# Reordering the fill of a two-layer graph kernel: small vectors' transpose, an affine step, half features, weight sums

## The chip, the cores and the metric

The kernel runs on one core of one Trainium2 chip. Its engines are TensorE (PE in the profile; PEld is its weight load), VectorE (DVE), ScalarE (ACT), GpSimd (POOL), and the DMA queues, of which SyncE (SP) issues most. The metric is the device time of one execution in microseconds (us). All line numbers are those of the kernel before; the changed kernel's run lower by one from line 588 on and drift further behind the edits.

## The reference

There are 64 graphs with 256 nodes and 256 features each (x), and a 0/1 adjacency matrix of 256 x 256 per graph. Two layers follow each other, everything in float32.

Layer 0: `h = gat(x, W1, a1)`, `h = gat(h, W2, a2)`, where `gat` projects `Wh = h @ W`, forms scores `leaky_relu(Wh @ a[:F] + (Wh @ a[F:]).T)` masked by the adjacency, takes a softmax over `axis=1`, and multiplies by `Wh`. Then `h = layernorm(x + h) * g + b`, `ff = relu(h @ w_ff1 + b_ff1) @ w_ff2 + b_ff2` with 1024 hidden values, and `layernorm(h + ff) * g + b`.

Layer 1: q, k from Wq, Wk, eight heads of 32, scores and a softmax; for each relation r of four, `out += (attn * (adj == r)) @ v_r` (with a 0/1 adjacency only relations 0 and 1 are ever selected); an output projection Wo, a residual and a layernorm; a gelu feed-forward of 1024 hidden values, a residual and a layernorm.

## The kernel before

**Staging.** The core takes two graphs at a time, a pair u of 32 (NG). A pair's rows lie as four blocks of 128 (T = 4; blocks 0 and 1 are the first graph of the pair, 2 and 3 the second). The main part is a loop of turns (`turn`, from L1276): turn u does the attention and second feed-forward of pair u, and beside it the layer 0 feed-forward of pair u+1 and the graph attention of pair u+2. Ahead of the loop stands the fill (L1613 to L1754), which brings pair 0 to the start of its attention and pair 1 to its first layernorm. It is written out by hand, and so is the order of instructions on PE, SP, DVE, ACT and POOL there (`manual_schedule`). Each engine works its queue in that order, and a wait at the head of a queue holds what is behind it. In turns with a following pair, PE, SP, DVE and ACT are ordered by hand too; POOL's place is then set by where its instructions stand, with some tied behind a mark (`behind`).

**Seven products for eight.** Large products are done with seven block products in place of eight (`hidden_seven` L909, `HiddenOut` L998, `Projections` L1047). Each needs sums of weights, made once by POOL (`made`, L628, one sum of two tiles per step), and sums or differences of data, made by DVE. Results pass through a PSUM bank to which a later product is added, so that the later one may only start when the earlier has been read: product 7 follows 6 in its bank, 6 follows 1, 4 follows 7, and 3 follows 5 (which itself takes the bank of 2 in the hidden layers and the projections). `taken` reads by a copy on ACT, or, where the place has begun, by an add on DVE (L948, L1079, L1036). In the step names of the fill a digit is a product, a or b a half of the hidden blocks, r, c, d and s an activation.

**Layernorm.** `moments` (L860) takes statistics on DVE, `norm` (L870) makes 1/std on POOL (rs, L877 and L878), `offsets` (L883) makes -mean/std on DVE (nm, L885), and `applied_norm` (L887) applies both on ACT (L895). The affine step with gain and bias (`affine`, L898: `times` L904, `plus` L907, both DVE) is put on the residual rows alone. For the features that the next product reads, gain and bias are folded into the weights: `scaled` (POOL, L646) multiplies the weights by the gain, and `shift_products` (L634) and `shift_added` (L640) bring the bias through the weights into the next bias. These need gains and biases as columns, so eight small vectors are loaded as 28 rows and transposed by PE in `columns` (L487; the transpose is L499, the copy L500).

**Features.** PE transposes rows to features in PSUM (`turned`, L512), and ACT or DVE copies them (`features`, L521). `with_ones` (L708) has POOL write ones into one feature row that carries the bias. A pair's features hold the first graph in columns 0 to 255 and the second in 256 to 511. `Projections.sums` (L1058) makes four differences from both graphs' features.

**Buffers.** Ordinary PSUM banks (`bank`, L423) turn in a ring of six.

**The order around the change.** At the head, PE transposes the small vectors (L588), then the first graph's adjacency (L1627), then alternates projections of pair 0 (`project`, L1631) with sums of the first bias through wf1 (L1632). ACT's queue begins with a check of the adjacency values (`checked`, L1625), which waits for that matrix's DMA. In the middle, the affine step of pair 0 (L1716) stands between two groups of sums; DVE does it ahead of the adds of product 6. At the end (L1745 to L1753) both graphs' rows are normed, transposed, copied as whole features, given their ones, and only then turn 0 begins with its differences and products.

Of the kernel before, what the change touches and what calls it, by code (L numbers as in the profile page):

```python
# [9 lines left out]
F32 = mybir.dt.float32  # L10
# [6 lines left out]
P = 128  # L17
# [368 lines left out]
def narrow_path(  # L386
# [13 lines left out]
    nc = tc.nc  # L400
# [4 lines left out]
    KB = F // P  # L405
# [81 lines left out]
    def columns(vs, name, queue, tag):  # L487

        ns = [v.shape[0] // P for v in vs]
        rows = work.tile([P, KB, TN], F32, tag=tag, name=f"{name}r", bufs=1)[:, 0, 0:P]  # L490
        t = const.tile([P, sum(ns)], F32, name=name)
        at, views = 0, []
        for v, n in zip(vs, ns):
            queue.dma_start(rows[at:at + n, :], v.rearrange("(c p) -> c p", p=P))
            views.append(t[:, at:at + n])
            at += n
        def turned_columns():
            ps = bank(f"{name}p")
            nc.tensor.transpose(ps[:, :at], rows[:at, :], ident[:at, :at])  # L499
            nc.vector.tensor_copy(t, ps[:, :at])  # L500
            return views

        return turned_columns
# [75 lines left out]
    def idle(n):  # L579
# [5 lines left out]
    idle(5)  # L585
    gwe = gat_weights()
    wf1 = weight(g_wf1, "wf1")
    lg1, lb1, bf1, lg2, lb2, lg3, lb3, b1 = columns(  # L588
        (g_g1, g_b1, g_bf1, g_g2, g_b2, t_g1, t_be1, t_b1), "cols", nc.scalar, "q")()

    wqk = const.tile([P, KB, 2 * F], F32, name="wqk")
    for k in range(KB):
# [35 lines left out]
    def made(ops, n=4):  # L628
        for _ in range(n):
            o, x_, y_, op = next(ops)  # L630
            nc.gpsimd.tensor_tensor(o, x_, y_, op)
# [63 lines left out]
    def behind(*names):  # L695

        stack = ExitStack()
        for n in names:
            stack.enter_context(tc.issue_after(mark[n].ins))
        return stack  # L700
# [346 lines left out]
    class Projections:  # L1047
# [3 lines left out]
        def __init__(s, u, hT):  # L1051
            s.u = u
            s.qk = work.tile([P, KB, 2, TN], F32, tag="q", name=f"qk{u}", bufs=1)
            s.v = work.tile([P, T, 2 * F], F32, tag="v", name=f"v{u}", bufs=1)
            s.h = [[hT[k][:, b * N:(b + 1) * N] for b in range(G)] for k in range(KB)]
            s.one, s.two, s.begun = {}, {}, set()

        def sums(s):  # L1058
            tt = work.tile([P, HPB, NB * N], F32, tag="e", name=f"tq{s.u}").rearrange("p a n -> p (a n)")
# [213 lines left out]
        if left:  # L1273
            next(left[0], None)

    def turn(y_, x_, z):  # L1276
        Y, X, Z = (g.get(u) for u in (y_, x_, z))
        hT, y = Y["hT"], Y["y"]
        quads = [(b, m) for b in range(G) for m in range(KB)]
# [40 lines left out]
        def moved(moves, n):  # L1320
            for _ in range(n):
# [2 lines left out]
        order = tc.manual_schedule(engines={getattr(mybir.EngineType, n) for n in  # L1324
                                            ("PE", "SP", "DVE", "Activation")[:4 if X else 2]})
        with order:
            p.sums()
            if X:
                n = X.pop("n")
                if y_:  # L1330
                    offsets(*n)
                p("q2 v2 q1 v1")
                if not y_:
                    offsets(*n)
                applied_norm(X["y"], *n, [0, 1, 2, 3])
                p("q5")
            else:
                p("q1 v1 q2 v2 q5")
# [113 lines left out]
                shares(1)  # L1452
            if not y_:
                with behind("low"):
                    made(w2m, 4)
            out_(0)
            if Z:
# [155 lines left out]
    with tc.manual_schedule(engines={getattr(mybir.EngineType, n) for n in  # L1613
                                     ("PE", "SP", "DVE", "Activation", "Pool")}):
        a, b = g[0], g[1]

        def spread(m):
            m.scores(0)
            m.scores(1)

        def powers(m):
            m.exp(0)
            m.exp(1)

        checked(0, g[0]["aq"], squares[:, 2:4].rearrange("p a n -> p (a n)"))  # L1625
        onlys = [only_row(n) for n in ("wqk", "wv")]
        turn_a = early_adjacency_of(0, 0)  # L1627
        turn_a()
        ps = bank("bf1sp")
        for t in range(T):  # L1630
            project(0, [t])  # L1631
            shift_products(ps, wf1, range(2 * t, 2 * t + 2), lb1)  # L1632
        shift_added(ps, range(FB), bf1)
        turn_a = early_adjacency_of(0, 1)
        turn_a()
        first_scores(0)
        spread(a["m"])
        powers(a["m"])
        turn_b = [early_adjacency_of(1, 0)]
        px = turned(b["y"], "xT1")  # L1640
        b["xT"] = features("xT1", px, (nc.scalar.copy,) * 2)
        pqk = row_products(wqk, "wqk", onlys[0])
        for k in range(G):
            a["m"].masks(k)
        a["m"].shares()
        a["m"].scaled(WH)
        scaled(wf1, lg1)
        made(wf1m, 2)
        first_sums(0)
        scaled_rows(wqk, *pqk)  # L1650
        nc.vector.tensor_tensor(wv[:, :, 1, :], wv[:, :, 1, :], wv[:, :, 0, :], ALU.subtract)
        second_scores(0)
        turn_b.append(early_adjacency_of(1, 1))
        spread(a["m"])
        a["m"].exp(0)
        project(1, range(NB))
        a["m"].exp(1)
        project(1, range(NB, T))
        for k in range(G):
            a["m"].masks(k)  # L1660
        a["m"].shares()
        made(wf1m, 2)
        made(wf2m, 1)
        first_scores(1)
        a["m"].scaled(F)
        for t in turn_b:
            t()
        second_sums(0, (0,))
        n0 = norm(0, 0, a["y"], range(NB))
        b["m"].raw(0)  # L1670
        b["m"].raw(1)
        checked(1, g[1]["aq"], squares[:, 2:4].rearrange("p a n -> p (a n)"))
        second_sums(0, (1,))
        mv = moments(0, 0, a["y"], range(NB, NB + 1))
        offsets(*n0)
        n1 = norm(0, 0, a["y"], range(NB, T), mv=mv, rest=range(NB + 1, T))
        applied_norm(a["y"], *n0, range(NB))
        offsets(*n1)
        applied_norm(a["y"], *n1, range(NB, T))
        b["m"].leaky(0)  # L1680
        pv = row_products(wvf, "wv", onlys[1])
        ph = turned(a["y"], "h1T0", range(NB))
        ps = bank("b1sp0")
        shift_products(ps, w1, range(0, 2), lb3)
        idle(2)
        turned(a["y"], "h1T0", range(NB, T), ph)
        shift_products(ps, w1, range(2, 4), lb3)
        a["hT"] = features("h1T0", ph, (nc.scalar.copy, nc.vector.tensor_copy))
        load_x(2)
        load_rows(2)  # L1690
        load_adjacency(2)
        steps = first_hidden(0)
        b["m"].leaky(1)
        shift_added(ps, range(0, 4), b1)
        steps("2a")
        powers(b["m"])
        steps("1a")
        b["m"].masks(0)
        steps("2b 1b")
        b["m"].masks(1)  # L1700
        b["m"].shares()
        for rb, v in shifts:
            nc.gpsimd.tensor_add(rb, rb, v)
        made(wf2m, 3)
        steps("5a 5b")
        b["m"].scaled(WH)
        scaled_rows(wvf, *pv)
        nc.vector.tensor_tensor(brow[:, 3], brow[:, 3], brow[:, 2], ALU.subtract)
        biased(wqk, brow[:, 0:2])
        biased(wvf, brow[:, 2:4])  # L1710
        made(wqkm, 4)
        steps("3a 3b")
        ps = bank("b1sp1")
        shift_products(ps, w1, range(4, 6), lb3)
        first_sums(1)
        affine(a["y"], rg1, rb1)  # L1716
        shift_products(ps, w1, range(6, FB), lb3)
        shift_added(ps, range(4, FB), b1)
        scaled(w1, lg3)
        made(w1m, 2)  # L1720
        steps("6a ra 6b rb")
        second_scores(1)
        steps("7a sa 7b sb 4a 4b")
        first = HiddenOut(0, 0, a["y"], a["h1"], wf2s, out_sums(0, 0))
        first.sums(1, 2)
        spread(b["m"])
        powers(b["m"])
        first(1)
        first.sums(4)
        first(2, 5)  # L1730
        b["m"].masks(0)
        first.sums(3)
        first(6)
        b["m"].masks(1)
        b["m"].shares()
        b["m"].scaled(F)
        made(wvm, 4)
        first(3)
        n0 = norm(0, 1, a["y"], range(NB))
        first(7)  # L1740
        offsets(*n0)
        applied_norm(a["y"], *n0, range(NB))
        first(4)
        n1 = norm(0, 1, a["y"], range(NB, T))
        second_sums(1, (0,))  # L1745
        ph = turned(a["y"], "h2T0", range(NB))
        offsets(*n1)
        applied_norm(a["y"], *n1, range(NB, T))
        second_sums(1, (1,))
        turned(a["y"], "h2T0", range(NB, T), ph)  # L1750
        mv = moments(1, 0, b["y"], range(NB))
        a["hT"] = with_ones(features("h2T0", ph, (nc.scalar.copy,) * 2))
        b["n"] = norm(1, 0, b["y"], mv=mv)  # L1753
        late.append((a["y"], rg2, rb2))  # L1754
    with tc.manual_schedule(engines={mybir.EngineType.PE, mybir.EngineType.SP}):
        for u in range(NG):
            turn(u, u + 1, u + 2)


    c = work.tile([P, 4], F32, tag="mv", name="checks")  # L1760
# [51 lines left out]
```

## Time and profile before

| | |
|---|---|
| three runs | 2962.96, 2960.92, 2951.9 us; median 2960.92 us |
| profiled execution | 2953.9 us, span 2952.3 us, granted PE clock 0.998 |
| PE busy | 2921.4 us, 99% of the span |
| DVE busy | 2612.6 us, 88% |
| ACT busy | 1898.3 us, 64% |
| POOL busy | 629.3 us, 21% |
| chain that ended last | PE 96%, DVE 2%, ACT 1% |

A busy PE is one with a matmul under way; matmuls are pipelined, so the sum of single durations is larger than the time they take together. The chain that ended last is followed back from the last instruction, at each step to what released it. Three parts of the span differ: the fill up to some 102 us, the turns, and the last turn from about 2850 us on, where fewer pairs are left to work beside each other. The change touches the fill and, by two weight sums, the first turn.

### The profile page before, as it was taken

The numbers are of one execution on the slowest core, as the hardware profiler recorded it, in microseconds if no ns is written. First come the engines' busy times: TensorE is split into PE (matmuls) and PEld (weight loads), VectorE is DVE, ScalarE is ACT, GpSimd is POOL, SyncE is SP. The second block draws the span as 40 slices with busy tenths as digits, with TensorE's granted clock in tenths as the row PEclk, the third lists the DMA queues.
The fourth block names the chain that finished last, engine by engine and source line by source line (L and its number), as shares of the span: only waits on it lengthen the run. The fifth ranks groups of instructions, "written<-read, shape, count | busy, mean of one in ns | idle before, by whom it ended". The sixth has DMA issues, their size and how long they took to land.

```text
span 2952.3 us, 58648 instructions
## 1 busy us (share of the span) xinstructions
PE 2921.4 (99%) x22206; PEld 2501.8 (85%) x22206; DVE 2612.6 (88%) x5027; ACT 1898.3 (64%) x3982; POOL 629.3 (21%) x930
## 2 busy tenths in 40 slices
PE   8999999999999999999999999999999999999997
PEld 7788888888888888888888888888888888888876
DVE  5889899989989898999898998899998989988987
ACT  5566666676676666666766766766667667667652
POOL 4212221122121122221221211222212212112211
PEclk9999999999999999999999999999999999999999
DMA  5011111111111111111111111111111111111000
GB/s 152 12 31 32 38 32 34 24 40 32 37 29 23 38 32 39 32 32 24 39 32 37 31 28 31 35 37 34 30 23 40 32 37 32 29 30 33 18 8 16
DMA packets 408020, 99.27 MB, mean 34 GB/s; under 512 B 357834, under 2 KB 407220, under 8 KB 407732
## 3 DMA queue, kind: packets, MB, share of 16 engines
q1 hardware_dynamic: 406332, 94.13, 14.8%
q8 instruction: 178, 2.92, 0.4%
q0 software_dynamic: 1056, 1.05, 0.1%
q14 instruction: 110, 0.90, 0.1%
q10 hardware_dynamic: 344, 0.28, 0.0%
HBM read 56.78 MB, written 16.78 MB: 25 GB/s over the span
## 4 chain that ended last, share of the span: by engine, by line
PE 96%; DVE 2%; ACT 1%; issue 0%; POOL 0%; DMA 0%; POOLq 0%; DVEq 0%; ACTq 0%
PE yf L1028 26%; PE h1a L939 15%; PE h1b L939 11%; PE po L1144 8%; PE v L1095 6%; PE qk L1095 6%; PE sp L1116 4%; PE hpp L840 4%; PE xpp L773 4%; PE ygp L851 4%; PE yop L851 4%; PE zo L1147 2%; PE rows L782 1%; DMA first<-in_adj_dram 0%; DVE st L866 0%
## 5 line engine op out<-in xcount | busy, mean ns | idle before, releaser
L1125 ACT ACTIVATE e<-sp 128x512 f32<-128x512 f32 x512 | 270.9, 611 | 71.4 <-issue 42.8
L1129 DVE TENSOR_TENSOR ea<-e,aT 128x1024 f32<-128x1024 f32 x256 | 310.9, 1216 | 1.8 <-ACT e L1125 1.8
L895 ACT ACTIVATE y<-y,nm,rs 128x256 f32<-128x256 f32 x442 | 235.1, 592 | 63.7 <-DVE nm L885 62.9
L948 DVE TENSOR_TENSOR h<-h1a,h 128x512 f32<-128x512 f32 x293 | 197.3, 682 | 80.7 <-PE h1a L939 77.3
L951 ACT COPY h<-h1b 128x512 f32<-128x512 f32 x293 | 175.2, 599 | 124.8 <-PE h1b L939 123.2
L957 ACT ACTIVATE h<-h,cols 128x256 f32<-128x256 f32 x512 | 221.9, 502 | 36.2 <-DVE h L948 32.0
L735 POOL COPY hT<-yt 32x256 f32<-32x256 f32 x244 | 211.5, 867 | 143.3 <-DVE yt L718 128.6
L1082 ACT COPY qk<-qk 128x512 f32<-128x512 f32 x128 | 74.4, 581 | 238.9 <-PE qk L1095 238.1
L866 DVE BATCH_NORM_STATS2 st<-y 128x6 f32<-128x256 f32 x512 | 208.6, 408 | 5.6
L877 POOL TENSOR_SCALAR rs<-mv 128x4 f32<-128x4 f32 (+1 forms) x134 | 41.5, 309 | 806.8 <-DVE mv L867 445.8
L1036 DVE TENSOR_TENSOR y<-yf,y 128x256 f32<-128x256 f32 x448 | 185.5, 414 | 30.5 <-PE yf L1028 30.5
L957 ACT ACTIVATE h<-h1a,cols 128x256 f32<-128x256 f32 x256 | 102.7, 464 | 131.8 <-PE h1a L939 131.8
L1157 POOL TENSOR_TENSOR low<-low,rq 128x16 f32<-128x16 f32 x64 | 14.0, 219 | 811.9 <-DVE rq L1156 811.9
L907 DVE TENSOR_TENSOR y<-y,rb 128x1024 f32<-128x1024 f32 x126 | 163.6, 1298 | 2.2
L1134 DVE TENSOR_TENSOR es<-e 128x1024 f32<-128x1024 f32 x128 | 155.8, 1217 | 0.0
L904 DVE TENSOR_TENSOR y<-y,rg 128x1024 f32<-128x1024 f32 x126 | 153.5, 1218 | 0.1
L878 POOL TENSOR_TENSOR rs<-rs,mhalf 128x4 f32<-128x4 f32 (+1 forms) x134 | 139.9, 1044 | 8.3
L939 PE MATMUL h1a<-tt,wf 128*128 128x256 f32 x512 | 137.7, 392 | 1.5 <-DVE h L948 1.5
L1116 PE MATMUL sp<-qk 32*128 32x256 f32 x2048 | 138.3, 394 | 0.0
L1144 PE MATMUL po<-e,v 128*32 128x256 f32 x2048 | 135.5, 382 | 0.0
L1144 PE MATMUL po<-ea,v 128*32 128x256 f32 x2048 | 134.4, 379 | 0.0
L718 DVE STREAM_TRANSPOSE yt<-y 128x256 f32<-128x256 f32 x364 | 128.3, 407 | 0.8 <-ACT y L895 0.7
(285 smaller groups left out, 7733.7 us busy)
## 6 DMA issues: line engine op xcount, KB each, us to landing
hT<-yt SPq DMA_DIRECT2D x666, 32.0 KB, 1.8
y<-in_x_dram SPq DMA_DIRECT2D x32, 512.0 KB, 4.2
xq<-in_x_dram SPq DMA_DIRECT2D x240, 64.0 KB, 2.1
aq<-in_adj_dram SPq DMA_DIRECT2D x240, 64.0 KB, 2.3
out_dram<-y SPq DMA_DIRECT2D x30, 512.0 KB
wf<-in_L_gnn_w_ff_dram SPq DMA_DIRECT2D x2, 1024.0 KB, 8.6
w<-in_L_gnn_W_dram SPq DMA_DIRECT2D x2, 1024.0 KB
first<-in_adj_dram POOLq DMA_DIRECT2D x2, 512.0 KB, 9.8
```

Of the source, the lines that this page charges most:

```text
L735: nc.gpsimd.tensor_copy(to, at)
L851: nc.tensor.matmul(ps[:, i * F:(i + 1) * F], lhs(t, k), rhs(b, k), start=(k == 0), stop=(k == n - 1))
L866: nc.vector.bn_stats(st[:, t, :], y[:, t, :])
L895: mark["normed"] = nc.scalar.activation(y[:, t, :], y[:, t, :], AF.Identity, bias=nm[:, t:t + 1], scale=rs[:, t:t + 1])
L939: nc.tensor.matmul(ps[:, i * N:(i + 1) * N], w_[:, f * P:(f + 1) * P], m, start=first and i == 0, stop=True, skip_group_check=True)
L957: nc.scalar.activation(y, y if ps is None else ps[:, i * N:(i + 1) * N], func, bias=bi[:, f:f + 1])
L1028: nc.tensor.matmul(s.ps[n][:, i * F2:(i + 1) * F2], a[:, k, i * P:(i + 1) * P], w_[:, k, :], start=n in (1, 2, 5) and i == 0 and k == 0, s ...
L1095: nc.tensor.matmul(ps[:, i * N:(i + 1) * N], l, r, start=n in (1, 2, 5) and i == 0, stop=True, skip_group_check=True)
L1116: nc.tensor.matmul(ps[a][:, j * N:(j + 1) * N], k_[hp, m, j0:j0 + P], q[hp, m, b * N:(b + 1) * N], start=True, stop=True)
L1125: nc.scalar.activation(e[:, a, :], ps[a], AF.Exp, scale=isd)
L1129: nc.vector.tensor_tensor(ea[:, a:a + 2, :], e[:, a:a + 2, :], ab[:, None, :].to_broadcast([P, 2, NB * N]), ALU.mult)
L1144: nc.tensor.matmul(po[hp, m * N:(m + 1) * N], vs[:, hp], w[:, a, j * N:(j + 1) * N], start=(n == 0), stop=(n == len(terms) - 1))
```

## The change

Seven edits:

1. The small vectors' DMAs are issued where they were, but their transpose now follows the first graph's adjacency transpose and the projections of blocks 0 and 1. The sums of the first bias come in two groups between the remaining projections, and the second half of them, with the add to the bias, behind the score rows.
2. The affine step of pair 0 follows product 7 and its activation.
3. The first block product of the first output (`first(1)`) and its add stand ahead of the second of the data sums.
4. Two of POOL's four sums of w1 leave the fill. The four are now made in turn 0: the first two in the place there where the last two stood, the last two ahead of those of w2.
5. Pair 0's second features are copied graph by graph (`half`): ACT copies both blocks of the first graph; of the second graph ACT copies one and DVE the other. The ones are written per graph.
6. The moments of pair 1 are split: one block ahead of the offsets of pair 0's second graph, three behind.
7. Turn 0 begins with products 1 of q, k and v, which read the first graph's features alone. Then come pair 1's `norm` and the second graph's transposes and copies (`second_half`), then products 2, then the four differences. `Projections.t` starts as an empty list so that products can run ahead of the differences.

```diff
-    lg1, lb1, bf1, lg2, lb2, lg3, lb3, b1 = columns(
-        (g_g1, g_b1, g_bf1, g_g2, g_b2, t_g1, t_be1, t_b1), "cols", nc.scalar, "q")()
+    wcols = columns((g_g1, g_b1, g_bf1, g_g2, g_b2, t_g1, t_be1, t_b1), "cols", nc.scalar, "q")
...
-            s.one, s.two, s.begun = {}, {}, set()
+            s.one, s.two, s.begun, s.t = {}, {}, set(), [None] * 4
...
-    def turn(y_, x_, z):
+    def turn(y_, x_, z, rest=None):
...
         with order:
+            if not y_:
+                p("q1 v1")
+                rest()
+                p("q2 v2")
             p.sums()
             if X:
                 n = X.pop("n")
                 if y_:
                     offsets(*n)
-                p("q2 v2 q1 v1")
-                if not y_:
+                if y_:
+                    p("q2 v2 q1 v1")
+                else:
                     offsets(*n)
...
                 with behind("low"):
+                    made(w1m, 2)
                     made(w2m, 4)
...
-        onlys = [only_row(n) for n in ("wqk", "wv")]
         turn_a = early_adjacency_of(0, 0)
         turn_a()
+        project(0, [0, 1])
+        lg1, lb1, bf1, lg2, lb2, lg3, lb3, b1 = wcols()
+        onlys = [only_row(n) for n in ("wqk", "wv")]
         ps = bank("bf1sp")
-        for t in range(T):
+        for t in range(NB, T):
+            shift_products(ps, wf1, range(2 * t - 4, 2 * t - 2), lb1)
             project(0, [t])
-            shift_products(ps, wf1, range(2 * t, 2 * t + 2), lb1)
-        shift_added(ps, range(FB), bf1)
         turn_a = early_adjacency_of(0, 1)
         turn_a()
         first_scores(0)
+        shift_products(ps, wf1, range(4, FB), lb1)
+        shift_added(ps, range(FB), bf1)
...
-        affine(a["y"], rg1, rb1)
         shift_products(ps, w1, range(6, FB), lb3)
         shift_added(ps, range(4, FB), b1)
         scaled(w1, lg3)
-        made(w1m, 2)
         steps("6a ra 6b rb")
         second_scores(1)
-        steps("7a sa 7b sb 4a 4b")
+        steps("7a sa 7b sb")
+        affine(a["y"], rg1, rb1)
+        steps("4a 4b")
         first = HiddenOut(0, 0, a["y"], a["h1"], wf2s, out_sums(0, 0))
-        first.sums(1, 2)
+        first.sums(1)
+        first(1)
+        first.sums(2)
         spread(b["m"])
         powers(b["m"])
-        first(1)
...
         ph = turned(a["y"], "h2T0", range(NB))
+        h2T = work.tile([P, KB, TN], F32, tag="hT", name="h2T0")
+        a["hT"] = [h2T[:, k] for k in range(KB)]
+
+        def half(b_):
+            ns = slice(b_ * N, (b_ + 1) * N)
+            nc.scalar.copy(h2T[:, 1, ns], ph[1][:, ns])
+            nc.gpsimd.memset(h2T[one, KB - 1, ns], 1.0)
+            (nc.scalar.copy, nc.vector.tensor_copy)[b_](h2T[:, 0, ns], ph[0][:, ns])
+
+        half(0)
+        mv = moments(1, 0, b["y"], range(1))
         offsets(*n1)
         applied_norm(a["y"], *n1, range(NB, T))
+        mv = moments(1, 0, b["y"], range(1, NB), mv)
         second_sums(1, (1,))
-        turned(a["y"], "h2T0", range(NB, T), ph)
-        mv = moments(1, 0, b["y"], range(NB))
-        a["hT"] = with_ones(features("h2T0", ph, (nc.scalar.copy,) * 2))
-        b["n"] = norm(1, 0, b["y"], mv=mv)
+
+        def second_half():
+            b["n"] = norm(1, 0, b["y"], mv=mv)
+            turned(a["y"], "h2T0", range(NB, T), ph)
+            half(1)
+
         late.append((a["y"], rg2, rb2))
...
-            turn(u, u + 1, u + 2)
+            turn(u, u + 1, u + 2, second_half)
```

## The prediction

> **What bounds the kernel now.** I read the page's busy shares, then the busy time by stretch, then TensorE's (PE's) waits, then each engine's timeline around each wait. The busy time by stretch of the kernel before (microseconds, then each engine's busy time):
>
> ```profile
> 14.00:28.00 14.00, 12.81 (x80) 10.53 (x81) 4.41 (x17) 7.48 (x17) 0.52 (x2) 1.00 1.00 346
> 28.00:62.00 34.00, 33.37 (x170) 27.28 (x169) 24.62 (x53) 21.86 (x50) 19.57 (x21) 1.00 0.41 78
> 62.00:78.00 16.00, 13.83 (x103) 12.68 (x103) 13.66 (x26) 8.28 (x18) 8.24 (x7) 1.00 0.00 1
> 78.00:90.00 12.00, 9.48 (x57) 7.70 (x57) 7.31 (x26) 4.96 (x10) 5.43 (x10) 1.00 0.00 0
> 90.00:102.00 12.00, 11.18 (x51) 8.96 (x50) 8.33 (x16) 7.85 (x17) 3.91 (x6) 1.00 0.07 18
> 102.00:110.00 8.00, 8.00 (x57) 6.06 (x56) 7.93 (x12) 6.69 (x13) 0.00 (x0) 1.00 0.00 1
> 110.00:1000.00 890.00, 890.00 (x6815) 766.07 (x6814) 801.33 (x1543) 585.78 (x1232) 193.19 (x283) 1.00 0.16 32
> ```
>
> From 102 us on PE never stands: 890.00 of 890 (the stretches to 2850 us lack 0.78 in all). Whatever the fill gains is therefore passed on whole to the end, and PE's matmuls are the same before and after. From 14 to 102 us PE stands for 1.19 + 0.63 + 2.17 + 2.52 + 0.82 = 7.3 us. That is the ceiling: 0.25% of the span. PE's waits, up to 110 us:
>
> ```profile
> PE colsp L499 <- ACT xT L535: 3.4, 1, 3.4
> PE qk L1095 <- POOL h2T L710: 1.6, 1, 1.6
> PE h1a L939 <- DVE h L948: 1.5, 1, 1.5
> ...
> PE yf L1028 <- DVE y L1036: 1.2, 2, 0.6
> PE qk L1095 <- ACT qk L1082: 0.8, 1, 0.8
> PE hpp L840 <- ACT xp L831: 0.8, 1, 0.8
> ```
>
> The change aims at the first three. The third is VectorE's (DVE's) doing; its timeline:
>
> ```profile
> 58.77 2.18 DVE L904 TENSOR_TENSOR y<-y,rg 128x1024 f32<-128x1024 f32 x1
> 61.05 1.56 DVE L907 TENSOR_TENSOR y<-y,rb 128x1024 f32<-128x1024 f32 x1
> 62.64 0.16 DVE L642 TENSOR_TENSOR cols<-cols,b1sp 128x4 f32<-128x4 f32 x1
> 62.72 1.28 DVE L948 TENSOR_TENSOR h<-h1a,h 128x512 f32<-128x512 f32 x2
> ```
>
> The two products' adds (L948) queue behind the affine step, 3.9 us, and product 7 needs the first. GpSimd's (POOL's) timeline:
>
> ```profile
> 59.83 1.70 POOL L631 TENSOR_TENSOR wqks<-wqk 128x256 f32<-128x256 f32 x1
> ...
> 68.45 2.13 POOL L631 TENSOR_TENSOR w1s<-w1s,w 128x512 f32<-128x512 f32 x1
> 78.14 0.20 POOL L820 TENSOR_TENSOR lowg<-lowg,z 128x4 f32<-128x4 f32 x1 [7.55 <-DVE z L819]
> 78.29 0.73 POOL L631 TENSOR_TENSOR wvs<-wv 128x256 f32<-128x256 f32 x1
> ```
>
> Equal 128x256 sums take 1.70 beside the affine step and 0.73 alone; four wvs sums queue behind z and ahead of the norm's rs.
>
> **What the Trainium skill says.** "SBUF — State Buffer", section "Who interferes with whom": a VectorE instruction with two SBUF inputs and a GpSimd one that reads SBUF block each other outright, whichever comes second. The trace agrees: times (L904) took 2.18 us beside POOL's sums and 1.23 at 96.07, with no sum beside it. "PSUM — Partial Sum Buffer", section "Engine vs sequencer instructions": the VectorE, ScalarE and GpSimd queues are strict FIFO, and matmuls start in program order. The trace agrees: L948's adds above. "Perfetto Trace Analysis", section "GPSIMD Instruction": a GpSimd span is unreliable, spacing from start to start is better. I use spacing: the wvs sums start at 78.29, 79.10, 79.91, 80.59, so four take 3.0 us.
>
> **Part 1: small vectors later.** The 3.4 us wait stays. Banks turn by six; the transpose (colsp) asks for the thirteenth and gets the bank of xT0p0, which ScalarE (ACT) copies at 13.79 to 14.35, behind its check on the adjacency (DMA landed at 11.27, table load, square). In the changed kernel the thirteenth bank is the adjacency transpose's, first in the queue, so PE starts at 14.41 again; projections read that copy too. Gain 0. Then come the adjacency transposes (0.49) and two projections (0.88 each), and colsp at 16.66. Its copy on DVE ended 0.47 after colsp's start (14.41 to 14.88), plus 0.06 to PE, against 0.17 of own work: a new wait of 0.36. Two of four groups of sums (0.79 each in the chain) now stand behind the score rows, so rows start at 22.54 - 1.58 + 0.36 = 21.32, 1.2 earlier. But the add of the sums (L642, 0.16) stays ahead of the first leaky step in DVE's queue and waits for them: rows end 21.76, + 1.58 = 23.34, so leaky starts at 23.55 and not 24.10. The softmax is 0.55 earlier and would release hpp at 27.26; PE, which before took 4.05 from rows' end to free (22.98 to 27.03), is free at 23.34 + 4.05 = 27.39. hpp at 27.4 and not 27.81: **0.4 gained**. Bounds: 0 (columns 0.4 later than reckoned) to 1.2 (the add not in the way). Until 61.9 PE is dense and only shifts.
>
> **Part 2: affine behind product seven** (in times of before). Rows end at 61.92. Product 6 ended at 60.70, its add without affine at 61.35, so product 7 starts at 62.0 and not 63.55: 1.5. POOL's chain, no longer blocked, ends its scaling of w1 near 64.8 (third wf2 sum 58.15 + 1.27, four sums 3.0, scaling 2.2); affine follows 7b's add (64.45) at 64.8 and takes 2 x 1.22, to 67.2. On DVE follow s1 to 68.4 (before 69.45), add 1, s2 to 69.95, two leaky, s4, adds 2 and 5 to 73.0, two masks, s3, add 6 to 75.2, two masks, z at 76.05 (before 78.06), at the row's durations without POOL (1.22, 0.69, 0.42): the w1 sums that slowed s1 and s2 (1.83, 2.18) are gone. PE runs products 1, 2, 5, 6 without a gap from 65.5; 3 waits for add 5 (73.05), 7 for add 6 (75.25), 4 for add 7, which stands behind add 3 and the moments, at 78.05 (before 79.94). The norm's offsets (nm) still come 4.4 after z, through POOL's queue (lowg, four wvs sums, rs): 80.5, not 82.48. **2.0 here.**
>
> **Part 3: half features first.** PE: product 4 to 79.85, ygp 1.73, half transposes to 82.2 (rows normed at 81.75), ygp to 83.9. ACT's two half copies (0.38 each) end at 83.0, so q1 and v1 (1.73) run 83.9 to 85.65, where PE stood for copies and memset. Offsets of the second graph come 2.9 after the first (82.48 to 85.40), at 83.4; rows normed by 84.7; second transposes 85.65 to 86.1, q2 and v2 to 87.8. Here the change adds a wait: DVE has the adds of q2 and v2 ahead of the four differences. v2's add ends 88.5, the first difference 88.9, and q5 waits till 88.95 (before 92.43: 3.5). The differences end at 90.1, graph one's nm at 90.25, ACT norms from 90.4 (before 93.48: 3.1). ACT is the bound then: its copies for q5 and q6 queue behind that norm and free the banks, so q7 starts at 98.00 - 3.1 = 94.9. From there PE was dense. **3.1 for parts 2 and 3**; bounds 1.5 (only the product 7 wait) to 5 (the copy wait gone too and ACT not late).
>
> **Part 4: weight sums moved.** In the fill they are counted above. In turn 0 two w1s sums take the old place, and two more run before w2's four: from 131.94 POOL needs six times 1.28, to 139.65, not 137.03. The norm's rs started at 138.18 and ended at 139.53, but nm came only at 141.09 in DVE's queue. New end of rs: 141.0. The cover is that 1.5; without it the cost would be 1.5. The last sum meets DVE's leaky (138.76), which may slip by 0.9; the adds behind end at 142.6 and PE needs them at 143.57, 1.0 of slack. I take 0.3 lost, bounds 0 and 1.
>
> **Sum:** 0.4 + 3.1 - 0.3 = 3.2 us. The profiled execution took 2953.9, around a span of 2952.3; it becomes 2950.7. It lies 7.0 below the median shown, and the three runs spread from 2951.9 to 2962.96. The mean of all four is 2957.4; less 3.2 that is **2954**.
>
> **Rivals.** *Stalls only move (20%).* For it: every DVE step is in one queue, and q5 and q7 still wait there or on ACT. If affine and scaling of w1 block each other as affine and wqks do now (3.74 for 2.44, 1.3 lost ahead of s1), and turn 0 takes its 1.0, some 1 remains: 2956.5. Against: POOL's earlier end at 64.8. *All waits go (12%).* All but the 0.4 ahead of 14.41: 6.9, so 2950.5. Against: ACT's norm of 2.07 ahead of the q5 copy stays. *Slower (5%).* In turn 0 POOL's six sums are each blocked as the one of 2.13 was: 12.8 from 131.94, rs ends at 146.1, nm 5.0 late with DVE's adds behind it; less the 1.0 of slack PE loses 4.0, more than the 3.5 won: 2958. It decides from 2.05 per sum. Against: from 131 to 138 DVE mostly reads PSUM or one SBUF input, and the four sums there took 1.28 each.
>
> **How the numbers follow.** The forecast has 60%, 3% are for what I don't see. Half a percent, about what a measurement of this kernel can tell from no change, is 14.8 us; every case lies inside it. The executions spread by 11 us, more than any case is worth, so they set the range: from 2951.9 - 6, 2946, to the highest with nothing gained, 2963. Faster by over 0.5% means below 2946.1: 5%. Slower means above 2975.7: 3%. The rest is 92%.
>
> **What would show it.** Right: PE's first transpose of adjacency near 14.4, still behind ACT's xT; a wait of 0.4 ahead of bf1sp; hpp near 27.4; no wait at h1a (L938); affine 1.2 + 1.2; q1 near 83.4 on the new clock; q5 and q7 waiting for DVE and ACT; first scores near 99.2 and not 102.69; rs in turn 0 at POOL's heels. Wrong: PE starting by 13 (then the columns' DMA, not the bank, was the wait), affine above 2 us again, or a PE gap near 140 us.

## The result, and the profile after

The changed kernel takes 2950.82 us (median of 14 runs, 2947.56 to 2957.75). The kernel before, measured beside it, takes 2960.85 us (14 runs, 2951.9 to 2963.27). The ratio is 0.9975, 95% interval 0.9964 to 0.9985. That is within half a percent, as forecast, and the median lies 3.2 us below the predicted 2954. The profiled execution took 2950.62 us around a span of 2949.0, where the prediction's sum gave 2950.7. It agrees almost to the digit, which is partly luck: its clock was halved for 3.4 us at the head, which cost 1.7; PE's gap at the head ended 0.9 earlier than before; and a further 0.8 came in the turns, as shown below.

Busy time by stretch of the changed kernel (span from:to, length, then busy time and instructions of PE, PEld, DVE, ACT and POOL, the granted PE clock, the DMA share and GB/s):

```profile
14.00:28.00 14.00, 13.72 (x77) 11.21 (x75) 3.44 (x15) 6.78 (x15) 0.20 (x1) 0.88 1.02 356
...
62.00:78.00 16.00, 15.35 (x117) 14.04 (x115) 14.89 (x29) 9.62 (x22) 4.69 (x7) 1.00 0.00 1
78.00:90.00 12.00, 10.32 (x57) 8.81 (x58) 8.06 (x24) 4.64 (x10) 5.57 (x11) 1.00 0.01 2
90.00:102.00 12.00, 10.99 (x68) 8.53 (x69) 9.47 (x16) 8.39 (x18) 2.62 (x4) 1.00 0.06 16
...
110.00:1000.00 890.00, 890.00 (x6802) 767.50 (x6791) 801.37 (x1543) 585.49 (x1233) 195.82 (x285) 1.00 0.16 32
```

From 62 to 78 us PE stands for 0.65 and not 2.17, from 78 to 90 for 1.68 and not 2.52; the loop is dense as before. In the first stretch PE looks fuller than before (13.72 against 12.81), but its clock is 0.88, and matmuls that run longer at the lower clock are counted as busy all the same (four of them, L772, take 1.57 at 19.09 and 1.12 at 17.32). PE's waits up to 110 us (engine and line waited for: sum, times, longest):

```profile
PE aTp L754 <- ACT xT L535: 2.6, 1, 2.6
...
PE qk L1094 <- DVE tq L1062: 1.2, 1, 1.2
PE yf L1027 <- DVE y L1035: 1.2, 3, 0.6
PE qk L1094 <- ACT qk L1081: 1.0, 2, 0.7
PE bf1sp L636 <- DVE cols L500: 0.3, 1, 0.3
```

The waits at product 7 (1.5), at POOL's ones (1.6) and at the first softmax (0.8) are gone. As the prediction named, q5 now waits behind the differences (1.2) and q7 behind ACT's copy; but this second one is no new wait, it was 0.8 before and is 0.7 of the 1.0 here. New is the 0.3 for the columns (predicted 0.36). The queues around q5 and q7 (start, busy time, engine):

```profile
88.64 0.69 DVE L1078 TENSOR_TENSOR v<-v,v 128x512 f32<-128x512 f32 x1 [0.16 <-PE v L1094]
89.25 0.42 DVE L1062 TENSOR_TENSOR tq<-h2T 128x256 f32<-128x256 f32 x1
...
90.78 0.16 DVE L884 SCALAR_TENSOR_TENSOR nm<-mv,rs 128x4 f32<-128x4 f32 x1
91.03 2.08 ACT L894 ACTIVATE y<-y,nm,rs 128x256 f32<-128x256 f32 x4 [3.76 <-DVE nm L884]
```

The first difference (tq) stands behind the add of v, the offset (nm) behind all four differences, and ACT's norm behind the offset. VectorE's timeline around the affine step (start, busy time, instruction):

```profile
63.39 0.69 DVE L947 TENSOR_TENSOR h<-h1a,h 128x512 f32<-128x512 f32 x1 [0.54 <-PE h1a L938]
64.25 0.69 DVE L947 TENSOR_TENSOR h<-h1a,h 128x512 f32<-128x512 f32 x1 [0.17 <-PE h1a L938]
64.86 1.77 DVE L903 TENSOR_TENSOR y<-y,rg 128x1024 f32<-128x1024 f32 x1
66.74 1.23 DVE L906 TENSOR_TENSOR y<-y,rb 128x1024 f32<-128x1024 f32 x1
```

The four adds go through and the affine step stands behind them. POOL's timeline, first in the fill, then in turn 0:

```profile
60.23 0.73 POOL L630 TENSOR_TENSOR wqks<-wqk 128x256 f32<-128x256 f32 x1
...
63.34 2.23 POOL L645 TENSOR_SCALAR w<-w,cols 128x1024 f32<-128x1024 f32 x2
...
135.70 1.27 POOL L630 TENSOR_TENSOR w2t<-w,w2t 128x512 f32<-128x512 f32 x1
136.93 0.68 POOL L876 TENSOR_SCALAR rs<-mv 128x4 f32<-128x4 f32 x1
```

Without the affine step beside them POOL's 128x256 sums take 0.73 each, not 1.70. In turn 0 the six sums take 1.27 each, and rs follows at their heels.

**Where the time went.** Because the clock disturbs the head of this execution, I count from the first softmax product (hpp), which starts at 27.81 before and 28.21 after; from there to 110 us the clock is 1.00 in both. "Gain" is by how much a step comes earlier after hpp.

| step | start before | start after | gain | predicted (parts 2, 3) |
|---|---|---|---|---|
| product 7 | 63.55 | 62.32 | 1.63 | 1.5 |
| product 4 | 79.94 | 78.50 | 1.84 | 1.9 |
| norm's offset nm | 82.48 | 81.03 | 1.85 | 2.0 |
| q5 | 92.43 | 89.72 | 3.11 | 3.5 |
| ACT's norm of pair 1 | 93.48 | 91.03 | 2.85 | 3.1 |
| first scores | 102.69 | 100.23 | 2.86 | 3.1 |

So some 2.9 us come from the middle and the end of the fill, against 3.1 predicted.

Behind the fill the gain isn't passed on quite unchanged. The first scores of the last turn but one start at 2803.23 before and 2799.94 after, with the clock at 1.00 in between, so there the gain after hpp is 3.69. The further 0.8 is net: turn 0 gives back 0.2, and four later turns are shorter by 0.1 to 0.4 each, in the profiles of r1 and b1 below as in this one. The profiles show no wait to which this can be put down; its cause stays open.

The medians, though, lie 10 us apart. The experiments look for the rest.

### The profile page after: what moved, and what is told of

It is laid out like the page before. It is cut to its first block, busy times and chain, and to the rows that moved or that the text cites. A ratio compares the mean times of both kernels' runs of the same rounds, so it can differ in the third digit from the quotient of the medians.

```text
span 2949.0 us, 58651 instructions
## 1 busy us (share of the span) xinstructions
PE 2921.7 (99%) x22206; PEld 2505.9 (85%) x22206; DVE 2611.3 (89%) x5028; ACT 1897.2 (64%) x3983; POOL 625.6 (21%) x931
## 3 DMA queue, kind: packets, MB, share of 16 engines
q1 hardware_dynamic: 406332, 94.13, 14.8%
q0 software_dynamic: 1056, 1.05, 0.1%
## 4 chain that ended last, share of the span: by engine, by line
PE 97%; DVE 2%; ACT 1%; DMA 0%; issue 0%; POOL 0%; DVEq 0%; POOLq 0%; ACTq 0%
PE yf L1027 27%; PE h1a L938 15%; PE h1b L938 11%; PE po L1143 8%; PE v L1094 6%; PE qk L1094 6%; PE sp L1115 4%; PE hpp L839 4%; PE ygp L850 4%; PE xpp L772 4%; PE yop L850 4%; PE zo L1146 2%; PE rows L781 1%; DMA first<-in_adj_dram 0%; DVE st L865 0%
```

## The experiments

**How they are read.** The times of one kernel lie in two groups, and the mean granted PE clock that comes with each execution tells them apart. The kernel before was run 130 more times: 61 of these had a clock of 0.994 to 0.996 and took 2961.6 us on average, 69 had 0.997 to 0.999 and took 2954.6. The median jumps from one group to the other: 2960.46 us (54 runs), 2955.75 (33) and 2955.71 (43) on three chips. I therefore give the median and ratio, and beside them the difference at equal clock: one straight line with a common slope through all executions of all kernels (2.43 us, plus or minus 0.08, for each 0.001 of mean clock), with a constant for each kernel. Intervals are 95%; since the clock is recorded to 0.001, up to 1 us more of uncertainty is possible. On this scale the changed kernel stands 4.0 plus or minus 0.5 below the kernel before. The groups say the same without a line: 2957.6 (3 runs) and 2950.1 (11 runs) for the changed kernel, 4.0 and 4.4 less.

### The changed kernel again, and its parts alone

Four kernels on one chip. `r1_after` is the changed kernel once more.

> The changed kernel again, beside the kernel before. Theory A (the fill's waits are what was won): at the same mean granted clock of TensorE the span is 2.5 to 4 us shorter than before, and nothing else differs. Theory B (the reordering also changes how often the clock is lowered): the medians differ by 7 us or more and the mean clocks differ as well; 0.001 of mean clock should be worth about 2.5 to 3 us whichever kernel it is. If the clock dip between 18 and 23 us that the profile of the changed kernel shows comes from the change, it is there again, and hpp begins near 28.2; if it is chance, this profile may lack it, and hpp begins near 27.4 when the adjacency lands as it did before.

`r2_vectors_only` is the kernel before with edit 1:

```diff
+        project(0, [0, 1])
+        lg1, lb1, bf1, lg2, lb2, lg3, lb3, b1 = wcols()
+        onlys = [only_row(n) for n in ("wqk", "wv")]
...
+        shift_products(ps, wf1, range(4, FB), lb1)
+        shift_added(ps, range(FB), bf1)
```

> The kernel before with the later transpose of the small vectors alone. Theory of the prediction: the first score rows 1.2 us earlier, hpp 0.4 us earlier relative to the start of the adjacency transposes, and 0.4 us in all. Rival (clock): the long run of one-column products leaves TensorE less busy, its clock is halved for some 3.4 us around 19 to 23 us, and the part loses about 1.3 us instead.

`r3_affine_w1_only` is the kernel before with edits 2, 3 and 4:

```diff
-        made(w1m, 2)
...
+        steps("7a sa 7b sb")
+        affine(a["y"], rg1, rb1)
+        steps("4a 4b")
```

> The kernel before with the affine step behind product 7, the first output product ahead of the second sum, and the weight sums moved, and nothing else. Theory of the prediction: the wait of 1.5 us at product 7 goes, the offsets of the first graph come 1.8 to 2.0 us earlier, and as the rest of the fill follows from them, 1.8 to 2.0 us in all at the same clock. Rival (the stalls only move): the affine step in front of the first data sum costs as much as it gave, less than 0.7 us in all.

`r4_half_only` is the kernel before with edits 5, 6 and 7:

```diff
+            if not y_:
+                p("q1 v1")
+                rest()
+                p("q2 v2")
```

> The kernel before with the features copied graph by graph and the first projections begun on one graph, and nothing else. Theory of the prediction: the 1.6 us wait for the ones goes but q5 waits for the adds of q2 and v2 and the differences, so 1.0 to 1.2 us in all at the same clock. Rival (all of it is won): the wait goes and nothing takes its place, 1.6 us or more and no wait at q5.

Measured, against 54 runs of the kernel before; the last column is the gain between hpp and the first scores in each profile (before: 74.88 us):

| kernel | median us (range, runs) | ratio | at equal clock | in the profile |
|---|---|---|---|---|
| r1_after | 2951.75 (2948.14 to 2959.36, 18) | 0.9980 [0.9971, 0.9988] | -3.8 ± 0.5 | 2.89 |
| r2_vectors_only | 2956.60 (2953.61 to 2964.26, 13) | 1.0001 [0.9991, 1.0011] | +0.2 ± 0.5 | 0.04 |
| r3_affine_w1_only | 2957.32 (2951.57 to 2961.36, 13) | 0.9994 [0.9984, 1.0003] | -2.1 ± 0.5 | 1.83 |
| r4_half_only | 2959.09 (2950.50 to 2960.43, 21) | 0.9989 [0.9981, 0.9997] | -1.4 ± 0.4 | 1.05 |

In r3's profile PE's clock is halved from 89.4 to 92.8 us, which cost 1.7; the 1.83 is the gain at product 1 of q just ahead of that (88.44, 88.87 before), so it isn't read at the first scores. What follows: the middle and the end of the fill are worth 1.8 and 1.05, and together the 2.9 of the changed kernel. They add, so the rival by which stalls only move is out. Edit 1 lies ahead of hpp, so the last column can't show it. From PE's first instruction after its gap at the head to hpp it is 14.54 us in r2, against 15.02 in r3 and 15.01 in r4, which have the old head and a like stretch of halved clock (some 14.3 to 17.8 us): 0.47. Some 0.1 of that may be the stretch's place, since it begins 0.3 ahead of PE's first instruction in r2 and 0.1 behind it in r3 and r4. Profiles without any such stretch are cleaner: 13.40 with the old head (before, and h1 below), 13.01 and 12.97 with edit 1 (s3 and g2 below), so 0.4 gained. By time alone r2 can't be told from the kernel before: a gain of 0.4 lies just outside its interval, and inside it only with the rounding of the clock. So this part rests on the traces.

The profile of r1 has two stretches of halved clock at the head (14.8 to 18.2 and 21.6 to 25.0 us), and hpp only at 30.69; the changed kernel's first profile had one (19.6 to 23.0). The rival expected for r2, a stretch at 19 to 23, isn't there. So the same kernel has these stretches in different places.

### The weight sums left in the fill

`s1_w1_in_fill` is the changed kernel without edit 4.

```diff
         scaled(w1, lg3)
+        made(w1m, 2)
...
-                    made(w1m, 2)
                     made(w2m, 4)
```

> The changed kernel with the two weight sums of w1 put back into the fill, and nothing else. Theory of the prediction: GpSimd's sums then fall beside the affine step and the first data sums, which block each other, so product 4 comes 1 to 1.5 us later than in the changed kernel and the gain at the same clock shrinks from 3.6 to some 2.3 us; in turn 0 the norm's 1/std starts when its moments arrive and not at GpSimd's heels. Rival (the sums cost nothing where they were): the gain stays within 0.4 us of the changed kernel's.

Measured: 2952.25 us (2950.23 to 2961.7, 22 runs) against 2955.75 before (33), ratio 0.9984 [0.9976, 0.9991]; at equal clock 1.6 ± 0.4 below before. Of the 3.9 that the changed kernel gains (the mean of its own row and r1's, 4.0 and 3.8) 2.3 are lost, more than the 1.3 expected. Among PE's waits in its profile there is one that neither kernel has:

```profile
PE yf L1027 <- DVE eq L1013: 1.5, 1, 1.5
```

VectorE's add of the affine step takes 2.11 us there, and the first sum behind it (eq) 2.28, beside two POOL sums of 2.12 and 2.13; in the changed kernel they take 1.23, 1.22. From hpp to the first scores it is 73.88 us, 1.86 more than in the changed kernel. That is all of r3's 1.83: moving the affine step without moving the weight sums only moves the stall from product 7 to the output's products. Moving the sums without the affine step wasn't tried. In turn 0 the two moved sums cost nothing: from its first scores to those of turn 1 it is 90.62 us with them (changed kernel) and 90.61 without (s1). It is 90.40 in the kernel before and in r4 and 90.63 in r3, so the 0.2 that turn 0 gives back comes with edits 2 and 3. PE's waits between 110 and 2850 us are 0.5 in the changed kernel and in the kernel before.

### What holds q5 and q7

`s2_early_difference` is the changed kernel with another order of VectorE's queue in turn 0: the first difference, the add of q2 and the norm's offset stand ahead of the add of v2.

```diff
-                p("q2 v2")
-            p.sums()
+                p.sums([0])
+                p("q2")
+                offsets(*n)
+                p("v2")
+                p.sums([1, 2, 3])
```

> The changed kernel with VectorE's order at the start of turn 0 alone altered: the first difference ahead of the add of q's product 2, the offsets of the other pair right behind that add, then the add of v's product 2 and the other differences. Theory of the prediction (q5 waits for VectorE's queue, q7 for ScalarE's norm behind the late offsets): q5 starts 1.0 to 1.2 us earlier, ScalarE's norm 2 us or more earlier, the wait at q7 goes, and 1.7 to 2.3 us are won over the changed kernel at the same clock. Rival (the features' copies or the ones bind, not the queue): less than 0.5 us.

Measured: 2950.03 us (2946.92 to 2958.58, 8 runs), ratio 0.9981 [0.9967, 0.9995]; at equal clock 6.2 ± 0.7 below before. From hpp to the first scores it is 69.55 us, 2.47 less than in the changed kernel, and PE waits neither at q5 nor at q7. So both waits came from the order in which VectorE worked off two adds, four differences and an offset; ACT was late at q7 only because the offset was.

### What holds PE at the head

`s4_check_behind` is the changed kernel with ACT's check of the adjacency behind the first two projections' copies.

```diff
-        checked(0, g[0]["aq"], squares[:, 2:4].rearrange("p a n -> p (a n)"))
         turn_a = early_adjacency_of(0, 0)
         turn_a()
         project(0, [0, 1])
+        checked(0, g[0]["aq"], squares[:, 2:4].rearrange("p a n -> p (a n)"))
```

> The changed kernel with ScalarE's check of the adjacency put behind the first two projections' copies, so that the copy of the first features no longer queues behind it. Theory of the prediction (the first transpose waits for the bank that ScalarE's copy of xT frees, and the small vectors were not what TensorE waited for): TensorE starts near 11 to 11.5 us, when the adjacency lands, and 2 to 3 us are won over the changed kernel, and the gap is too short for a lower clock. Rival (the small vectors' or the first weights' transfer binds): the wait only moves to the small vectors' transpose or to the first one-column product, and less than 1 us is won.

Measured: 2947.62 us (2946.67 to 2948.6, 6 runs), ratio 0.9968 [0.9956, 0.998]; at equal clock 6.8 ± 0.8 below before, some 2.9 more than the changed kernel's 3.9. PE's first adjacency transpose starts at 11.44, and the small vectors' own transpose at 13.75, neither behind a wait that the profile shows. That settles the prediction's reading of the 3.4 us: PE stood for a bank that ACT had to empty behind its check and the table load with it, and not for the small vectors.

```profile
11.44 0.63 PE L754 MATMUL aTp<-ident,first 128*128 128x128 f32 x4
13.75 0.24 PE L499 MATMUL colsp<-ident,colsr 28*128 28x28 f32 x1
```

### PE's gap at the head, and its clock

The profiles of s1 and s2 happen to show an execution of the other group (mean clock 0.995 and 0.994). Busy time by stretch of s1, columns as above:

```profile
11.00:14.00 3.00, 0.21 (x1) 0.00 (x0) 0.43 (x1) 2.62 (x4) 0.00 (x0) 0.88 0.80 208
14.00:18.00 4.00, 3.57 (x11) 2.99 (x12) 0.00 (x0) 1.34 (x3) 0.00 (x0) 0.50 0.90 292
...
30.00:34.00 4.00, 4.00 (x20) 4.00 (x21) 2.18 (x8) 1.56 (x4) 0.00 (x0) 0.50 0.48 129
34.00:38.00 4.00, 4.00 (x8) 1.87 (x7) 0.83 (x5) 2.46 (x6) 2.78 (x4) 0.60 0.74 124
```

After its gap PE works from 14.43 on nearly without a pause, yet the clock stays at 0.50 until some 37 us, 24 us in all. The matmuls really are slow: the projection of one block takes 2.08 us there and 1.12 in the kernel before. hpp starts at 38.22 instead of 27.81. The mean agrees: 24 us at half clock take 24 x 0.5 / 2960 = 0.0041 off it, and 4.1 x 2.43 is 10.0 us. The groups lie some 7 us apart; of the executions with a clock of 0.994 to 0.996 only these two left a trace, so the stretches of the others may be shorter, and that they have one is read from their mean clock alone.

`s3_busy_head` is the changed kernel with four extra 128x256 products in PE's gap; nothing reads what they give.

```diff
         checked(0, g[0]["aq"], squares[:, 2:4].rearrange("p a n -> p (a n)"))
+        zi = psum.tile([P, 512], F32, tag="zo", name="warm")
+        for _ in range(4):
+            nc.tensor.matmul(zi[:, 0:N], gwe[:, KB - 1, 0:P], gwe[:, KB - 1, 0:N], start=True, stop=True)
```

> The changed kernel with four extra products (of a weight tile with itself, their result not used) where TensorE stands before the first adjacency transpose. Clock theory: the halved clock at 14 to 17 us follows that gap; with it filled the clock stays whole up to 60 us, the mean clock rises by 0.0005 to 0.001 over the changed kernel's 0.997, and hpp begins near 27.4 after a start near 14.4, or as much earlier as the adjacency lands earlier. Rival (the dip is chance or comes from the one-column products): a dip of the same length stays between 14 and 25 us and the mean clock is as in the changed kernel.

Measured: 2949.19 us (2948.21 to 2951.57, 10 runs), ratio 0.9973 [0.9963, 0.9982]; at equal clock 3.6 ± 0.6 below before, like the changed kernel, but no execution below a clock of 0.997. To separate this from edit 1, `h1_before_head_filled` puts the same four products into the kernel before, ahead of its small vectors' transpose, which is called behind them for that.

```diff
         checked(0, g[0]["aq"], squares[:, 2:4].rearrange("p a n -> p (a n)"))
+        zi = psum.tile([P, 512], F32, tag="zo", name="warm")
+        for _ in range(4):
+            nc.tensor.matmul(zi[:, 0:N], gwe[:, KB - 1, 0:P], gwe[:, KB - 1, 0:N], start=True, stop=True)
+        lg1, lb1, bf1, lg2, lb2, lg3, lb3, b1 = wcols()
         onlys = [only_row(n) for n in ("wqk", "wv")]
```

> The kernel before with four extra 128x256 products in the gap of PE at the head, ahead of the transpose of the small vectors; their result is not used. No other wait changes, so at equal clock it stands where the kernel before stands (0, within 1). Clock theory: the gap is what lets PE's clock fall by half for some 24 us in about half of the executions of the kernel before; with the gap filled no execution has a mean clock of 0.994 to 0.996, and the median is near 2953 instead of 2960. Rival: the gap has nothing to do with it, the clock falls by chance or because of a later load; then half of the executions still lie at 2959 to 2963 and the median stays within 3 of that of before.

Measured: 2953.3 us (2951.47 to 2955.73, 22 runs) against 2955.71 before (43), ratio 0.9988 [0.9982, 0.9995]; at equal clock 0.5 ± 0.4 below before. None of the 22 has a clock below 0.997, while 17 of the 43 of the kernel before do, on the same chip. In its profile PE's gap is in pieces, the longest 0.9:

```profile
PE colsp L499 <- ACT xT L535: 0.9, 1, 0.9
```

The transpose starts at 14.52 and hpp 13.40 us after it, the same 13.40 as before. So the four products shorten nothing that the profile shows; what they take away is the executions at 0.994 to 0.996, and so, by the two traces, the long stretch of halved clock. The rival, chance or a later load, is out.

`b1_no_vectors` is the changed kernel without edit 1, to see whether that edit makes the stretch rarer.

```diff
-        project(0, [0, 1])
-        lg1, lb1, bf1, lg2, lb2, lg3, lb3, b1 = wcols()
-        onlys = [only_row(n) for n in ("wqk", "wv")]
         ps = bank("bf1sp")
-        for t in range(NB, T):
-            shift_products(ps, wf1, range(2 * t - 4, 2 * t - 2), lb1)
+        for t in range(T):
             project(0, [t])
+            shift_products(ps, wf1, range(2 * t, 2 * t + 2), lb1)
+        shift_added(ps, range(FB), bf1)
```

> The changed kernel without edit 1 alone: the small vectors' transpose stands ahead of the adjacency's again, and all sums of the first bias between the projections. At equal clock it loses the 0.4 to 0.5 of part 1 against the changed kernel, so it stands some 3.3 below the kernel before. If edit 1 is also what makes the long stretch of halved clock rarer, some half of the executions have a mean clock of 0.994 to 0.996 and the median lies near 2956 (between 2950 and 2958); if that rarity comes from any other edit, or from the chips used, a quarter or fewer have it and the median lies near 2951.

Measured: 2955.84 us (2947.57 to 2958.44, 22 runs), ratio 0.9988 [0.998, 0.9997]; at equal clock 3.6 ± 0.4 below before. The 0.4 that edit 1 is worth can't be seen at this precision, but 12 of the 22 executions have a clock of 0.995 or 0.996, against 7 of 32 of the changed kernel. All kernels together, executions at 0.994 to 0.996:

| head of the kernel | kernels | executions |
|---|---|---|
| as before | before, r3, r4, b1 | 92 of 186 |
| edit 1 | after, r1, r2, s1, s2 | 18 of 75 |
| gap filled or shortened | s3, s4, g2, h1 | 0 of 44 |

Fisher's exact test gives 0.0002 for the first row against the second and 0.0001 for the second against the third. On the one chip that ran r1 to r4 it is 48 of 88 and 8 of 31 (0.007). So edit 1 halves the share, and without PE's gap there is none. How edit 1 does it isn't settled: the gap is no shorter (2.6 us in the profiles of the changed kernel and of b1 alike). What it changes is what follows the gap. There the old head has narrow products of one column (128x1) between the projections, and the new one doesn't at first; whether that matters wasn't tried.

### A version better than both

`g2_both` is the changed kernel with s2's order and s4's.

> The changed kernel with both changes at once that the runs before tried singly: ACT's check of the adjacency behind the first two projections' copies (s4_check_behind), and turn 0's queue of VectorE with the first difference and the norm's offset ahead of product 2 of v (s2_early_difference). Theory: the two sit in different stretches of a fill whose gains pass whole to the end, so they add: at equal clock the changed kernel gained 4.0 over the kernel before, s4 2.9 more and s2 2.4 more, together some 9 less than before; and since PE's gap ahead of the first transposes is gone, no execution with the long stretch of halved clock: median near 2945, mean clock 0.997 or more in all. In the trace hpp near 26, no PE wait at q5 and q7, and first scores (sp) some 69.5 after hpp. Rival: ACT is the common bound at q7, so that what s4 brings earlier is given back at a new wait behind ACT's norm: then no more than 7 at equal clock, and a PE wait of 1 or more between q5 and the first scores.

Measured: 2944.35 us (2943.56 to 2944.39, 6 runs), ratio 0.9954 [0.9938, 0.9969]; at equal clock 9.4 ± 0.8 below before, clock 0.998 or 0.999 in all. PE's waits up to 110 us are only these:

```profile
PE idle L583 <- DVE squares L577: 1.4, 1, 1.4
PE yf L1027 <- DVE y L1035: 1.1, 3, 0.6
PE bf1sp L636 <- DVE cols L500: 0.3, 1, 0.3
PE ygp L850 <- ACT hp L830: 0.2, 1, 0.2
PE aTp L754 <- DMA first<-in_adj_dram: 0.2, 1, 0.2
```

The two add: 3.9 + 2.9 (s4) + 2.3 (s2) = 9.1. hpp starts at 24.32, and the first scores 69.64 us later. The expectation had 26 for hpp; that number came from s4, whose profile has a stretch of halved clock from 17 to 21 us (hpp at 26.09), which this one lacks. At the head PE now waits for the adjacency's own DMA.

## Why the prediction was right, and what it missed

**Class and sum.** Within half a percent was right, for the reason given: PE's idle time in the fill is 7.3 us, a quarter of a percent, and the rest of the span passes a gain on, though not quite unchanged: the turns add the 0.8 whose cause is open. The 3.2 us of the sum are borne out for the fill: 0.4 + 1.83 + 1.05 = 3.3 in the profiles. With the 0.8 of the turns it is 4.1, and at equal clock the changed kernel and r1 measure 4.0 and 3.8.

**Part 1: 0.4; found 0.4.** The mechanism holds. The wait at the head stays, behind ACT's copy, and s4 shows that the bank behind the check was its cause. PE started at 13.54 in the profiled execution and at 14.33 in r1's, around the 14.41 expected. "hpp near 27.4" missed (28.21), because the clock was 0.70 and 0.87 between 18 and 26 us, and "first scores near 99.2" (100.23) with it. In s3, where PE starts at 14.41 and no such stretch follows, hpp is at 27.42.

**Part 2: 2.0; found 1.83.** Product 7 no longer waits, and the chain from it to the norm came as forecast. "Affine 1.2 + 1.2" was a little low: 1.77 + 1.23, while POOL's scaling of w1 (63.34, 2.23 long) still ran when the affine step began at 64.86. And the prediction didn't part the credit: it put the 2.0 down to the affine step's place and named the w1 sums only among the reasons why later sums get faster. s1 shows that without moving these sums nothing of the 1.8 remains.

**Part 3: 1.1 of the 3.1; found 1.05.** q5 waits for the differences and q7 for ACT, as written. But "ACT is the bound then" holds for this order of VectorE's queue alone: in s2, with ACT's norm as long as before (2.08) but earlier, q7 doesn't wait, and 2.5 more are won. So the bound of 5 was within reach.

**Part 4: -0.3; found 0 for the sums.** rs came at POOL's heels and VectorE's leaky step slipped by 0.5 (1.81 for two against 1.28), inside the 0.9 that was allowed. The slack behind it took that up, as s1's equal turn shows. The rival of six blocked sums fails at its own threshold: 1.27 each, not 2.05.

**The step that failed** is the last one of the sum, "the mean of all four is 2957.4; less 3.2 that is 2954". It took the spread of the executions for noise that a change in the fill leaves alone. It is PE's clock, and edit 1 changes how often that falls for up to 24 us: 7 of 32 executions instead of about half. The median therefore moved by 10.0 us: some 4 at equal clock, and the other 6 from the middle of the distribution going over from one group to the other. The number came within 3.2 us and inside the range, but by a sum that lacked this term.

## What to carry to other kernels

When executions differ by more than a change is worth, set the granted clock of each beside its time before comparing medians; here two groups 7 us apart hid gains of 1 to 4 us and made one look like 10. A gap of PE near the start can cost far more than its own length, and a few spare matmuls in it are cheap insurance. Before moving a VectorE step, look at what GpSimd does beside its new place: here the affine step's move was worth nothing unless two weight sums left as well.

## What was not expected of the hardware

In s1 PE was busy for 19.3 of the 20 us from 14 to 34, yet its clock, halved from some 13 us on, came back only at some 37. The Trainium skill, page "TensorE: Matmul & The Clock Gate", section "What's actually happening", says that the clock halves after an idle window of about 3.4 us, that one busy window of the same length brings it back, and that the windows run freely, so that executions differ. The length of the window shows in the traces: the stretch of lowered clock at the head comes to 3.4 us in the changed kernel (19.6 to 23.0 us), s4 and b1, worked out as the sum of each slice's length times (1 - clock) / 0.5, and to 23.9 us in s1 and s2, seven times 3.4. One busy window does not fit these seven. And s4 has its one short stretch (17.4 to 20.8) though PE had no gap over 0.3 us from 8 us on.

Nor did the length of PE's wait decide: with 3.40 the clock stayed at 1.00 in the profile of the kernel before, with 4.05 r1 had only short stretches, with 2.85 s2 had the long one. In s1 and s2 the clock fell only some 2.1 us after PE's last product ahead of the gap (at 13.3 and 13.4 us; the gap begins at 11.2 and 11.3). The same page's section "HAM oscillation — how this bites in real kernels" advises against gaps over about 3.4 us; here 2.85 was enough, and with waits of at most 1.1 in the profiles of h1 and s3 none of their 32 executions had a mean clock below 0.997. The measurements decide: in this kernel such a gap can cost 7 to 10 us.
